# Three moves in a one-core latent-attention kernel: later hooks, another fetch order, and a step's first keys made one step earlier

## The chip, the core and the metric

The kernel runs on one core of a Trainium2 chip. Its time is the device time of one execution in microseconds (us), and less is better. The core has five engines with an instruction queue each: TensorE (PE in the profile, with its weight loads as PEld), VectorE (DVE), ScalarE (ACT), GpSimd (POOL) and SyncE (SP), which here only issues DMAs. A queue is worked off in order, so an instruction that waits holds up all that are behind it on the same engine.

## What is computed

The state x holds 8 batches of 64 tokens with 256 features (512 tokens), float32. The context holds 8 batches of 1601 rows with 128 features. Four levels follow each other, and each adds a cross attention to the context, a self attention and a feed-forward part to the state:

```python
x = x + L0_xattn(layernorm(x), ctx)   # attention a1 over x, an MLP, attention a2 over the context (16 heads of 32), an MLP
x = x + L0_attn(layernorm(x));  x = x + L0_ffn(layernorm(x))     # mixture of 8 experts
x = x + L1_xattn(layernorm(x), ctx, ctx)                         # one head of 256
x = x + L1_attn(layernorm(x));  x = x + L1_ffn(layernorm(x))     # a recurrence; 8 experts with a capacity
x = x + L2_xattn(layernorm(x), ctx)                              # 16 heads of 64
x = x + L2_attn(layernorm(x));  x = x + L2_ffn(layernorm(x))     # mixture of 8 experts
x = x + L3_xattn(layernorm(x), ctx)                              # 16 heads of 16
x = x + L3_attn(layernorm(x));  x = x + L3_ffn(layernorm(x))     # mixture of 16 experts
```

The attention in the first one normalises the context rows, then takes for every head the softmax over the 1601 rows:

```python
yn = _ln(y, lny_g, lny_b)                       # y is the context; per row
a = softmax(einsum('bhsd,bhtd->bhst', q, k) * D ** (-0.5))
o = einsum('bhst,bhtd->bhsd', a, v)             # k and v are projections of yn
```

The last one (L3) is `Q = x @ Wq.T`, `K, V = z @ Wkv.T` of the raw context z, softmax over 1601 keys per head, and `O @ Wo.T`.

## The kernel before

**The stages** follow each other as the reference does. In the texts below, the *first cross attention* is a2 (131 to 568 us), the *second* is x1 (L1, 780 to 840), the *third mixture* is f2 (L2's experts, 1487 to 1581), and the *third cross attention* whose keys the change speaks of is x3 (L3, 1581 to 1897), which the code does with `narrow_attention`. (Between the second one and x3 stands x2 of L2, 990 to 1436, which the change leaves alone.)

**The turned loop** (`turned_attention`) does a2, x2 and x3. It lays keys on partitions and 512 columns (heads times tokens) on the free axis. A batch has 13 key tiles of 128 rows (the last has 65), in pairs 7 chunks (`NCK`), and two halves of the heads, so that a batch takes 14 steps and the whole loop 112 and some more to run out. In step s it does, in this order: the hooks of that step (own work of the stage, given as a dictionary from step to functions), the shift (L808, DVE) and the exponential (L812, ACT) of older chunks, the scores of chunk s (L865, four TensorE records into two one-bank PSUM tiles psS, each copied to SBUF by ScalarE as raw, L866) with a running maximum on VectorE (top, L787), and the sums of the chunk that is `LATE` = 10 steps old (L877, TensorE, 16 records). After a half's last chunk the maximum is turned (psm, L793), reduced (nm, L795) and spread over the keys again (psmb, L802; copy mb, L804, on ScalarE); the shift needs mb. The first sums can run only when the first half's maximum is known. That stretch, some 20 us from step 7 on, is called the fill below. The order is written out by hand (`tc.manual_schedule` on PE, ACT and DVE): the program's order is the order of those queues. POOL and SP go by a scheduler.

**a2's hooks** (L1508 to L1522) prepare batch b+1 while batch b runs, from step 14b on: `stats` in steps 0 to 4 (VectorE), `scales` in step 4 (POOL), `normalise` (L1394, ScalarE, four key tiles of the context in natural layout, cn, in place) in steps 7 to 10, `turn_context` (four TensorE transposes into psc, L1480, and ScalarE's copy to ct, L1482) in steps 9 to 12, the DMA `fetch` of batch b+2 in step 10, and, for two batches at a time (odd b), `ask` in step 12: TensorE's 32 products of the queries with the key weights (psqk, L918), copied by ScalarE (qk, L935). psc, psqk, psm, psmb and the turned answers all come from one PSUM pool `ps` with two buffers. The answers of a half are turned (psot, L898; copy oT, L901) and, per batch, multiplied by the value weights (pso, L1503; copy into qT, L1506).

**x1** (the loop `flash`) takes two batches as a tile, with both layouts of the context (cn natural, ct turned) loaded for each: `fetch(i)` issues cn, ct, cn, ct on SP for tile i, and is called for tile i+1 in tile i's second unit. Scores (L1684) read ct, the sums read cn. The buffers are 4 of each, so two tiles.

**f2** ends with the shared expert's last product (psd, L1140; added to X, L1288) and `collect` (L1283 to L1285): four reads of the answers from DRAM (got, alternately issued by SP and ScalarE), and eight additions into X on VectorE. Weights come by `weight(name)` into a ring of six slots (L314 to L318); a load waits until the slot's last reader is done, so adding a load to the ring changes which reader each later load waits for, and the loads are issued by SP in order.

**x3** takes xn, turns it (L384), projects the queries (psl, L402, copied to qT by ScalarE and VectorE), and then `narrow_attention` sets the value tiles v to one (L949, POOL), loads the turned context of two batches (ct), spreads the queries of batch 0 (`ask`, qz, L957, POOL) and makes the keys of the first half (`key_part(0, n)`, psk, L965, copy kT, L966), all ahead of the loop. Other halves' keys are made by hooks in the loop. Here the loop has one score buffer (psS with four banks, L988, copied by L993) and `late` is 11. The answers go to a tile oT, which the last product (`lin_nat`) reads.

Of the kernel before, what the change touches and what calls it, by code (L numbers as in the profile page):

```python
# [11 lines left out]
F32 = mybir.dt.float32  # L12
# [5 lines left out]
P = 128  # L18
B, S, C = 8, 64, 256
NT = B * S  # L20
# [253 lines left out]
def perceiver(ctx: ExitStack, tc: tile.TileContext, d, col_at, row_at, const_at, out):  # L274
# [46 lines left out]
    def chunks(w, n):  # L321
        return w.rearrange("p (k n) -> p k n", n=n)
# [613 lines left out]

    def narrow_attention(ps, psS, psO, pool, q, wkv, outT):

        hm = K("hp16")
        cts, qzs, kTs, oas = {}, {}, {}, {}
        nk = -(-M // 4)
        vs = [pool.tile([P, KT * 4, 4, 16], F32, tag=f"v{n}", name="v", bufs=1) for n in range(2)]
        for v in vs:
# [99 lines left out]
        fetch(0)  # L1048
        fetch(1)
        ask(0)  # L1050
        for n in range(4):
            key_part(0, n)
        turned_attention(ps, pool, score_part, sum_part, hooks, LATE + 1, 4)


# [57 lines left out]

    def gated_parts(ps, pool, srcT, wg, wu, n, bg=None, bu=None):
        nh = -(-n // P)
        hT = pool.tile([P, nh, NT], F32, tag=f"hT{nh}", name="hT", bufs=1 if nh > 3 else 2)
        kc = C // P
        sgs = tpool.tile([P, 2, NT], F32, tag="T", name="sg")

        def up(c):  # L1120
            m = min(P, n - c * P)
            tg = ps.tile([P, 512], F32, tag="ps", name="psg")
            tu = ps.tile([P, 512], F32, tag="ps", name="psu")
            for w, t in ((wg, tg), (wu, tu)):
                for k in range(kc):
                    nc.tensor.matmul(t[:m], w[:, k, c * P : c * P + m], srcT[:, k, :], start=k == 0, stop=k == kc - 1)  # L1126
            sg = sgs[:, c % 2, :]
            if bg is None:
                nc.scalar.activation(sg[:m], tg[:m], AF.Silu)
                nc.vector.tensor_tensor(hT[:m, c, :], sg[:m], tu[:m], ALU.mult)  # L1130
            else:
                nc.scalar.activation(sg[:m], tg[:m], AF.Silu, bias=bg(c))
                nc.vector.scalar_tensor_tensor(hT[:m, c, :], tu[:m], bu(c), sg[:m], ALU.add, ALU.mult)

        def down(wd, done, tiles=range(NI)):
            for i in tiles:
                t = ps.tile([P, 512], F32, tag="ps", name="psd")
                for c in range(nh):
                    m = min(P, n - c * P)
                    nc.tensor.matmul(t[:, :C], hT[:m, c, i * P : (i + 1) * P], wd[:m, c, :], start=c == 0, stop=c == nh - 1)  # L1140
                done(i, t[:, :C])

        return up, down
# [188 lines left out]
    with tc.tile_pool(name="l0res", bufs=1) as res, ExitStack() as both:  # L1332
# [129 lines left out]
        with tc.tile_pool(name="a2o", bufs=1) as op:  # L1462

            qT = op.tile([P, 4, NT], F32, tag="qT", name="qT")
            with ExitStack() as _:
# [5 lines left out]
                with ps as ps, psS as psS, psO as psO, fp as fp:  # L1471
# [39 lines left out]
                    for b in range(B - 1):  # L1511
                        at = 2 * NCK * b
                        more = {k: [lambda b=b, k=k: stats(b + 1, 3 * k)] for k in range(5)}
                        more[4].append(lambda b=b: scales(b + 1))
                        for k in range(4):
                            more[7 + k] = [lambda b=b, k=k: normalise(b + 1, 4 * k)]
                        for k in range(4):
                            more.setdefault(9 + k, []).append(lambda b=b, k=k: turn_context(b + 1, 4 * k))
                        more[10].append(lambda b=b: fetch(b + 2))
                        if b % 2:  # L1520
                            more[12].append(lambda b=b: ask(b + 1))
                        hooks.update({at + k: v for k, v in more.items()})  # L1522
                    ask(0)
                    for k in range(0, KT, 4):
                        turn_context(0, k)
# [125 lines left out]
    with tc.tile_pool(name="x1", bufs=1) as pool:  # L1651
# [17 lines left out]
        with ps as ps, psS as psS, psO as psO, fp as fp:  # L1669
            ctx_of = {}  # L1670

            def fetch(i):
                for j in range(2):
                    cn = fp.tile([P, KT, CO], F32, tag="cn", name="cn", bufs=4)
                    nc.sync.dma_start(cn.rearrange("p k c -> p (k c)"), d["cn"][2 * i + j])
                    ct = fp.tile([P, M], F32, tag="ct", name="ct", bufs=4)
                    nc.sync.dma_start(ct, d["ct"][2 * i + j])
                    ctx_of[2 * i + j] = cn, ct

            def tile_of(i):  # L1680
                def scores(lo, hi, t):
# [266 lines left out]


    W2 = d["f2w"].shape[2]  # L1950
    weights2 = ExitStack()
    w2 = weights2.enter_context(tc.tile_pool(name="w2", bufs=1)).tile([P, 8 * W2], F32, tag="w2", name="w2")
    wq, wk, wvo = (chunks(weight(k), C) for k in ("b2q", "b2k", "b2vo"))
# [6 lines left out]
    with general() as ps, tc.tile_pool(name="f2", bufs=2) as pool:  # L1960
        wg = chunks(weight("f2g"), 8)
        ww = chunks(weight("f2s"), C)
        b2 = pool.tile([8, C], F32, tag="b2", name="b2", bufs=1)
        nc.sync.dma_start(b2, d["f2b"])
        xn = normed(X)
# [30 lines left out]
        with tc.manual_schedule(engines=FLASH):  # L1996
# [2 lines left out]
                (mybir.EngineType.PE, mybir.EngineType.DVE),  # L1999
            )  # L2000
        down(ww[:, 4:6], into_X, (1, 2, 3))
        collect(pool, shares)
    weights2.close()

    with tc.tile_pool(name="x3", bufs=1) as pool:
        wq, wkv, wo = (weight("x3" + k) for k in ("q", "kv", "o"))
        qT = pool.tile([P, 2, NT], F32, tag="qT", name="qT")
        oT = pool.tile([P, 2, NT], F32, tag="oTall", name="oTall")  # L2010
        with general() as ps:
            xT = transposed(ps, normed(X))
            lin_T(ps, chunks(wq, C), xT, C, lambda c, t: evac(qT[:, c, :], t))
        ps, psS, psO, fp = turned_pools("x3", 1, 1, 3)
        with ps as ps, psS as psS, psO as psO, fp as fp:
            narrow_attention(ps, psS, psO, fp, qT, wkv, oT)
        with general() as ps:
            lin_nat(ps, chunks(wo, C), oT, into_X)

# [68 lines left out]
```

## Time and profile before

| what | value |
| --- | --- |
| median of 3 runs | 2035.22 us (2032.83 to 2038.2) |
| profiled execution | 2034.59 us, of which the span is 2032.8 |
| busy over the span | PE 1836.7 us (90%), DVE 1236.9 (61%), ACT 1037.4 (51%), POOL 270.9 (13%) |
| mean granted TensorE clock | 0.951 |
| a2, 131 to 568 us | PE busy 421.75 of 437 us, ACT 299.76, DVE 296.46 |
| x1, 780 to 840 us | PE busy 49.10 of 60 us, DMA share 0.70 |
| f2, 1487 to 1581 us | PE busy 72.11 of 94 us |
| x3, 1581 to 1897 us | PE busy 278.71 of 316 us, DVE 272.28, ACT 269.40 |

Times of instructions are those of one profiled execution, counted from the start of its span. A line of the timeline gives start, duration, engine, line of the kernel, operation, output and inputs, their shapes, and how many instructions of one kind in a row it stands for; in brackets, how long the engine had been idle before and what released it. "Granted clock" is the share of full speed at which TensorE was clocked.

### The profile page before, as it was taken

What the parts mean: (1) busy time and instruction counts of PE and PEld (TensorE: products, weight loads), DVE (VectorE), ACT (ScalarE), POOL (GpSimd) and SP (SyncE); (2) the same over time, 40 slices, a digit from 0 to 9 for tenths busy, and PEclk for the clock granted to TensorE, in tenths of its full rate; (3) what the DMA queues carried; (4) which work ended last, traced back from release to release, by engine and by line L of the source; (5) the groups of instructions that cost most, each with busy time, mean ns of one, the idle gap of its engine ahead of it and who ended that gap; (6) DMA issues with size and microseconds to landing.
All of it is one profiled execution on the core that took longest, in us unless ns stands there. A gap on an engine that the chain in (4) does not pass through costs nothing.

```text
span 2032.8 us, 35983 instructions
## 1 busy us (share of the span) xinstructions
PE 1836.7 (90%) x14950; PEld 1350.3 (66%) x14950; DVE 1236.9 (61%) x2124; ACT 1037.4 (51%) x1721; POOL 270.9 (13%) x331
## 2 busy tenths in 40 slices
PE   6888999999989898769999999999969699998889
PEld 5546777777768475439657777778845377776747
DVE  6457676766726433661266666665544589999743
ACT  2347777777622222402166555555212499999323
POOL 3431010111022221000000000000122110100124
PEclk9999999999998898869999999999979799999989
DMA  8310000000005206317301010100421110100323
GB/s 309 116 62 1 18 18 18 18 28 1 1 25 219 89 29 269 113 44 256 133 17 34 34 34 34 34 18 7 191 81 40 68 35 19 35 19 17 141 67 106
DMA packets 38227, 142.24 MB, mean 70 GB/s; under 512 B 4936, under 2 KB 17872, under 8 KB 32496
## 3 DMA queue, kind: packets, MB, share of 16 engines
q1 hardware_dynamic: 32448, 127.98, 17.6%
q0 software_dynamic: 3696, 10.11, 1.4%
q8 instruction: 119, 1.95, 0.4%
q10 hardware_dynamic: 1920, 1.84, 0.3%
q14 instruction: 44, 0.36, 0.1%
HBM read 129.28 MB, written 19.71 MB: 73 GB/s over the span
## 4 chain that ended last, share of the span: by engine, by line
PE 66%; DVE 15%; ACT 8%; issue 2%; POOL 2%; DMA 1%; DVEq 0%; ACTq 0%; SPq 0%; POOLq 0%
PE psav L877 17%; PE psS L865 16%; PE psgd L1242 4%; DVE raw L808 4%; DVE top L787 4%; PE psl L402 3%; PE psn L411 2%; PE psy L1263 2%; ACT raw L993 2%; PE psg L1126 2%; PE psh L1867 1%; ACT raw L812 1%; PE psy L1871 1%; PE psu L1126 1%; ACT cn L1394 1%
## 5 line engine op out<-in xcount | busy, mean ns | idle before, releaser
L877 PEld LDWEIGHTS psav<-cn,raw 128*128 128x128 f32 (+1 forms) x3328 | 402.3, 191 | 87.1 <-issue 85.8
L808 DVE TENSOR_TENSOR raw<-raw,mb 128x1024 f32<-128x1024 f32 (+1 forms) x336 | 381.8, 1140 | 62.6 <-ACT mb L804 62.6
L877 PE MATMUL psav<-cn,raw 128*128 128x129 f32 (+1 forms) x3328 | 406.7, 275 | 0.7 <-ACT raw L812 0.7
L865 PE MATMUL psS<-qk,ct 128*128 128x512 f32 (+1 forms) x832 | 396.1, 598 | 7.6 <-ACT raw L866 7.6
L787 DVE TENSOR_TENSOR top<-raw,top 128x1024 f32<-128x1024 f32 (+1 forms) x240 | 267.9, 1116 | 135.6 <-ACT raw L866 111.9
L812 ACT ACTIVATE raw<-raw 128x1024 f32<-128x1024 f32 (+1 forms) x336 | 334.6, 998 | 14.3 <-DVE raw L808 11.9
L866 ACT COPY raw<-psS 128x512 f32<-128x512 f32 (+1 forms) x416 | 236.0, 585 | 132.0 <-PE psS L865 128.7
L865 PEld LDWEIGHTS psS<-qk,ct 128*128 128x128 f32 (+1 forms) x832 | 138.0, 187 | 114.5 <-issue 80.6
L993 ACT COPY raw<-psS 128x1024 f32<-128x1024 f32 (+1 forms) x112 | 106.6, 952 | 4.9 <-PE psS L988 4.8
L988 PE MATMUL psS<-qz,kT 32*128 32x128 f32 (+1 forms) x1664 | 78.0, 298 | 22.6 <-ACT raw L993 22.4
L1242 PE MATMUL psgd<-w,xdT 128*128 x272 | 91.9, 470 | 1.6 <-DVE xdT L1231 1.6
L475 POOL MEMSET vz<- 128x528 f32 (+1 forms) x12 | 7.4, 644 | 612.8 <-PE pso L1924 428.8
L781 DVE TENSOR_TENSOR top<-raw 128x1024 f32<-128x1024 f32 x48 | 58.7, 1222 | 46.1 <-ACT raw L866 35.7
L353 POOL TENSOR_TENSOR mv<-mv,mhalf 128x1 f32<-128x1 f32 x76 | 43.2, 572 | 325.6 <-DVE mv L352 315.0
L988 PEld LDWEIGHTS psS<-qz,kT 32*128 32x128 f32 (+1 forms) x1664 | 55.6, 183 | 46.5 <-ACT raw L993 38.3
L1007 PE MATMUL psav<-raw,v 128*32 128x64 f32 (+1 forms) x3328 | 71.9, 227 | 3.5 <-ACT raw L812 1.8
L804 ACT COPY mb<-psmb 128x512 f32<-128x512 f32 x48 | 28.1, 586 | 75.2 <-PE psmb L802 68.5
L1007 PEld LDWEIGHTS psav<-raw,v 128*32 128x32 f32 (+1 forms) x3328 | 53.5, 112 | 18.4 <-issue 3.3
L974 PEld LDWEIGHTS psv<-w_x3kv_None,ct 128*128 128x128 f32 (+1 forms) x416 | 54.0, 190 | 15.8 <-issue 3.1
L1268 POOL DMA_INDIRECT answered<-rows,homes x53 | 51.0, 963 | 95.5 <-ACT rows L1266 58.8
L1242 PEld LDWEIGHTS psgd<-w,xdT 128*128 128x128 f32 x272 | 48.2, 192 | 21.1 <-issue 8.8
L974 PE MATMUL psv<-w_x3kv_None,ct 128*128 128x128 f32 (+1 forms) x416 | 59.5, 282 | 0.0
(423 smaller groups left out, 2718.9 us busy)
## 6 DMA issues: line engine op xcount, KB each, us to landing
cn<-in_cn_dram SPq DMA_DIRECT2D x24, 838.5 KB, 4.4
ct<-in_ct_dram SPq DMA_DIRECT2D x24, 800.5 KB, 4.5
dealt<-in_deal_dram SPq DMA_DIRECT2D x3, 2955.5 KB, 26.9
w<-in_f0w_dram SPq DMA_DIRECT2D x8, 1088.0 KB, 14.8
w_f1up<-in_f1up_dram SPq DMA_DIRECT2D x8, 1024.0 KB, 4.8
w_f1dn<-in_f1dn_dram SPq DMA_DIRECT2D x8, 1024.0 KB, 4.9
w<-in_f2w_dram SPq DMA_DIRECT2D x8, 1024.0 KB, 14.1
w<-in_f3w_dram SPq DMA_DIRECT2D x16, 384.0 KB, 8.2
```

The lines of the kernel that those rows point to most:

```text
L402: nc.tensor.matmul(t[:m, :NT], w[:, k, c * P : c * P + m], src[:, k, :], start=k == 0, stop=k == kc - 1)
L787: nc.vector.tensor_tensor(top[:n, :m, :], raw, top[:n, :m, :], ALU.max)
L808: nc.vector.tensor_tensor(raw, raw, halves[h]["mb"][:n].unsqueeze(1).to_broadcast([n, m, 512]), ALU.add)
L812: nc.scalar.activation(raw, raw, AF.Exp)
L865: nc.tensor.matmul(x[:n], ct[:, kt * P : kt * P + n], qk, start=True, stop=True)
L866: nc.scalar.copy(raw[:n, i, :], x[:n])
L877: nc.tensor.matmul(oa[:, j // 2, j % 2 * CO : (j % 2 + 1) * CO], w[:n, i, j * P : (j + 1) * P], cn[:n, kt, :], start=kt == 0 and j % 2 == ...
L974: nc.tensor.matmul(t[:n, i * P : (i + 1) * P], cts[b][:, kt * P : kt * P + n], wkv[:, C + c * P : C + (c + 1) * P], start=True, stop=True)
L988: nc.tensor.matmul(x[:n, g, i * P : (i + 1) * P], kTs[h][r, kt * P : kt * P + n], qzs[b][r, c].rearrange("p m s -> p (m s)"), start=True, ...
L993: nc.scalar.copy(raw[:n, :m, :].rearrange("p i (g s) -> p i g s", g=4), x[:n, :, : m * P].rearrange("p g (i s) -> p i g s", s=P))
L1007: nc.tensor.matmul(oa[32 * g : 32 * g + 32, s * S : (s + 1) * S], vs[h % 2][:n, 4 * kt + g, 2 * s : 2 * s + 2, :].rearrange("p s d -> p (s ...
L1242: nc.tensor.matmul(y[:, :m], st[t]["xT"][:, k, :], w[:, bass.ds(x + at + k * m, m)], start=k == 0, stop=k == C // P - 1)
```

## The change

The change has three parts. In a2, the hooks `normalise` and `turn_context` are put three steps later (10 to 13 and 12 to 15 of a batch, so that the last two turns fall in the next batch's first two steps, and the hooks of a step are now extended instead of overwritten). In x1, `fetch` issues both ct of a tile ahead of both cn. For x3, the weights x3kv and the turned context of batch 0 are loaded into the weight ring at the start of f2, the keys of the first half are made at the end of f2, ahead of `collect`, into a tile kT0 of a pool of its own (`early`), and `narrow_attention` takes kT0 in place of making them; it still loads batch 0's context for itself, for the values and the second half's keys. The answers are written into qT itself and the tile oT goes. In `gated_parts` the tile hT has one buffer always, where it had two for f2.

```diff
--- before.py
+++ after.py
@@ -936,13 +936,13 @@
-    def narrow_attention(ps, psS, psO, pool, q, wkv, outT):
+    def narrow_attention(ps, psS, psO, pool, q, wkv, outT, kT0):
         hm = K("hp16")
-        cts, qzs, kTs, oas = {}, {}, {}, {}
+        cts, qzs, kTs, oas = {}, {}, {0: kT0}, {}
         nk = -(-M // 4)
         vs = [pool.tile([P, KT * 4, 4, 16], F32, tag=f"v{n}", name="v", bufs=1) for n in range(2)]
         for v in vs:
@@ -1048,8 +1048,6 @@
         fetch(0)
         fetch(1)
         ask(0)
-        for n in range(4):
-            key_part(0, n)
         turned_attention(ps, pool, score_part, sum_part, hooks, LATE + 1, 4)
@@ -1113,7 +1111,7 @@
     def gated_parts(ps, pool, srcT, wg, wu, n, bg=None, bu=None):
         nh = -(-n // P)
-        hT = pool.tile([P, nh, NT], F32, tag=f"hT{nh}", name="hT", bufs=1 if nh > 3 else 2)
+        hT = pool.tile([P, nh, NT], F32, tag=f"hT{nh}", name="hT", bufs=1)
         kc = C // P
         sgs = tpool.tile([P, 2, NT], F32, tag="T", name="sg")
@@ -1513,13 +1511,14 @@
                         more = {k: [lambda b=b, k=k: stats(b + 1, 3 * k)] for k in range(5)}
                         more[4].append(lambda b=b: scales(b + 1))
                         for k in range(4):
-                            more[7 + k] = [lambda b=b, k=k: normalise(b + 1, 4 * k)]
+                            more[10 + k] = [lambda b=b, k=k: normalise(b + 1, 4 * k)]
                         for k in range(4):
-                            more.setdefault(9 + k, []).append(lambda b=b, k=k: turn_context(b + 1, 4 * k))
+                            more.setdefault(12 + k, []).append(lambda b=b, k=k: turn_context(b + 1, 4 * k))
                         more[10].append(lambda b=b: fetch(b + 2))
                         if b % 2:
                             more[12].append(lambda b=b: ask(b + 1))
-                        hooks.update({at + k: v for k, v in more.items()})
+                        for k, v in more.items():
+                            hooks.setdefault(at + k, []).extend(v)
                     ask(0)
                     for k in range(0, KT, 4):
                         turn_context(0, k)
@@ -1670,12 +1669,14 @@
             ctx_of = {}
             def fetch(i):
-                for j in range(2):
-                    cn = fp.tile([P, KT, CO], F32, tag="cn", name="cn", bufs=4)
+
+                cts = [fp.tile([P, M], F32, tag="ct", name="ct", bufs=4) for _ in range(2)]
+                cns = [fp.tile([P, KT, CO], F32, tag="cn", name="cn", bufs=4) for _ in range(2)]
+                for j, ct in enumerate(cts):
+                    nc.sync.dma_start(ct, d["ct"][2 * i + j])
+                for j, cn in enumerate(cns):
                     nc.sync.dma_start(cn.rearrange("p k c -> p (k c)"), d["cn"][2 * i + j])
-                    ct = fp.tile([P, M], F32, tag="ct", name="ct", bufs=4)
-                    nc.sync.dma_start(ct, d["ct"][2 * i + j])
-                    ctx_of[2 * i + j] = cn, ct
+                    ctx_of[2 * i + j] = cn, cts[j]
             def tile_of(i):
                 def scores(lo, hi, t):
@@ -1948,6 +1949,8 @@
     W2 = d["f2w"].shape[2]
+    early = ExitStack()
+    kT0 = early.enter_context(tc.tile_pool(name="x3e", bufs=1)).tile([P, M], F32, tag="kT0", name="kT0")
     weights2 = ExitStack()
     w2 = weights2.enter_context(tc.tile_pool(name="w2", bufs=1)).tile([P, 8 * W2], F32, tag="w2", name="w2")
     wq, wk, wvo = (chunks(weight(k), C) for k in ("b2q", "b2k", "b2vo"))
@@ -1960,6 +1963,8 @@
     with general() as ps, tc.tile_pool(name="f2", bufs=2) as pool:
         wg = chunks(weight("f2g"), 8)
         ww = chunks(weight("f2s"), C)
+        wkv3 = weight("x3kv")
+        ct0 = weight("ct", 0)
         b2 = pool.tile([8, C], F32, tag="b2", name="b2", bufs=1)
         nc.sync.dma_start(b2, d["f2b"])
         xn = normed(X)
@@ -1999,23 +2004,30 @@
                 (mybir.EngineType.PE, mybir.EngineType.DVE),
             )
         down(ww[:, 4:6], into_X, (1, 2, 3))
+
+        for lo in range(0, M, 401):
+            n = min(401, M - lo)
+            t = ps.tile([P, 512], F32, tag="ps", name="psk")
+            nc.tensor.matmul(t[:, :n], wkv3[:, :P], ct0[:, lo : lo + n], start=True, stop=True)
+            nc.scalar.copy(kT0[:, lo : lo + n], t[:, :n])
         collect(pool, shares)
     weights2.close()
     with tc.tile_pool(name="x3", bufs=1) as pool:
-        wq, wkv, wo = (weight("x3" + k) for k in ("q", "kv", "o"))
+        wq, wo = (weight("x3" + k) for k in ("q", "o"))
         qT = pool.tile([P, 2, NT], F32, tag="qT", name="qT")
-        oT = pool.tile([P, 2, NT], F32, tag="oTall", name="oTall")
         with general() as ps:
             xT = transposed(ps, normed(X))
             lin_T(ps, chunks(wq, C), xT, C, lambda c, t: evac(qT[:, c, :], t))
         ps, psS, psO, fp = turned_pools("x3", 1, 1, 3)
         with ps as ps, psS as psS, psO as psO, fp as fp:
-            narrow_attention(ps, psS, psO, fp, qT, wkv, oT)
+            narrow_attention(ps, psS, psO, fp, qT, wkv3, qT, kT0)
         with general() as ps:
-            lin_nat(ps, chunks(wo, C), oT, into_X)
+            lin_nat(ps, chunks(wo, C), qT, into_X)
+
+    early.close()
```

## The prediction

> **What bounds the kernel now.** I read the chain of waits first, then busy time by stage, then TensorE's waits inside the stages that the edits touch, and last the timelines at the three places.
>
> ```profile
> PE 66%; DVE 15%; ACT 8%; issue 2%; POOL 2%; DMA 1%; DVEq 0%; ACTq 0%; SPq 0%; POOLq 0%
> ```
>
> TensorE carries two thirds of the chain, so an edit pays only where TensorE stands still. The windows (name, then length and the busy time of PE, weight loads, DVE, ACT and POOL, the granted clock, the DMA share, GB/s) show where that is:
>
> ```profile
> 131.00:165.00 34.00, 25.88 (x100) 12.29 (x99) 16.91 (x38) 23.00 (x46) 5.11 (x4) 0.95 0.04 16
> 215.00:482.00 267.00, 262.60 (x1741) 195.05 (x1741) 187.75 (x305) 190.16 (x331) 31.26 (x20) 1.00 0.06 19
> 1573.00:1597.00 24.00, 8.08 (x18) 3.28 (x16) 11.19 (x27) 1.13 (x2) 7.78 (x6) 0.64 0.34 118
> 1597.00:1621.00 24.00, 19.64 (x228) 13.61 (x228) 11.87 (x12) 17.61 (x27) 2.36 (x4) 1.00 0.09 32
> 1621.00:1627.00 6.00, 4.33 (x57) 3.57 (x56) 5.08 (x5) 5.33 (x6) 0.00 (x0) 0.57 0.00 0
> ```
>
> The first cross attention (131 to 568) loses 8.1 us of TensorE in its first 34 us and only 4.4 in the 267 us of its steady state. Ahead of the third cross attention's loop (1573 to 1597) 16 of 24 us are idle. TensorE's waits over the first cross attention (total, times, longest):
>
> ```profile
> PE psS L865 <- ACT raw L866: 5.9, 8, 2.4
> PE psqk L918 <- ACT qk L935: 2.4, 4, 0.8
> PE psqk L918 <- DVE qT L1506: 0.9, 3, 0.3
> ```
>
> The 5.9 are one wait of 1.49, one of 2.40 and six of 0.33: TensorE waiting for ScalarE to empty a score buffer. So the hooks' place matters, but what is to be had is some 6 us.
>
> **Part 1, later hooks in the first cross attention.** No instruction is added or removed; per batch the four normalisations go from steps 7–10 to 10–13 and the four turns from 9–12 to 12–15. Statistics (DVE), scales (POOL), the DMA fetch and the question stay in their steps. Where they lie now, on ScalarE and then on TensorE:
>
> ```profile
> 154.50 1.65 ACT L1394 ACTIVATE cn<-cn,cmv 128x128 f32<-128x128 f32 x4 [3.74 <-DVE nm L795]
> 156.99 0.58 ACT L804 COPY mb<-psmb 128x512 f32<-128x512 f32 x1
> 162.46 1.28 ACT L812 ACT_TABLE_LOAD   x1
> ```
>
> ```profile
> 154.53 0.65 PE L802 MATMUL psmb<-const,nm 128*128 128x128 f32 x4 [0.78 <-DVE nm L795]
> 165.33 1.98 PE L865 MATMUL psS<-qk,ct 128*128 128x512 f32 x4 [2.40 <-ACT raw L866]
> ```
>
> In the fill (the first half's softmax, when nothing older can be summed), ScalarE normalises from 154.50 although psmb is done at 155.18; mb, which releases the whole shift, comes at 156.99. Two more normalisations of 1.65 and a turn copy of 0.76 stand ahead of the table load at 162.46. Without them: mb 155.2–155.8, the shift (DVE 1.22) to 157.0, step 8's copies to 157.2, table load to 158.5, exponential (1.06) to 159.5, step 9's copies to 160.4. The first copy ends early enough that step 10's scores start near 160.0 instead of 165.33: −5.3. Two sets of turning transposes lay in TensorE's idle time there (159.40 and 162.33) and come later, on the path, at 0.44 each (their spacing): +0.9. Net −4.4. Ends: −5.3 if they find idle time again, −3.0 if only the two waits go (1.49 + 2.40 − 0.9).
>
> Steady state: per step TensorE has scores 1.72 and sums 1.79 (3.5, spacings), 0.44 more with a turn. ScalarE has an exponential and two copies (about 2.0), 1.55 more with a normalisation, 0.77 with a turn or an answer's copy. The six stalls of 0.33 stand in step 10 of a batch, where a normalisation, a turn and that copy meet; after, the normalisations of steps 10 to 13 meet 3.5 to 4.1 us of ScalarE work against 3.5 to 4.5 of TensorE's. I take the stalls as gone, −2.0, with 0 as the other end.
>
> The question in step 12 of three batches (224, 330 and 436 us) is what pays for it. Before, ScalarE reaches it with a lead: at 224.12 the last, short turn copy (0.41) had waited 1.43 for TensorE. After, a normalisation (1.55) and a full turn copy (0.77) stand ahead of it on ScalarE, the turn's psc and the question's psqk share two PSUM buffers, and TensorE's queue is in order: the scores of step 12 wait behind the question. Extra work ahead: 1.55 + 0.36 = 1.9; if the lead of 1.43 were still there, 0.5 would show; if it is gone, 1.9. Steps 10 and 11 now have a normalisation each, so the lead is mostly gone: 1.4 each, +4.2 (ends +1.5 and +5.7).
> Part 1: −4.4 − 2.0 + 4.2 = **−2.2**.
>
> **Part 2, fetch order in the second cross attention.** Of each pair of batches both ct are issued ahead of both cn. The queue moves 410 to 430 GB/s without a gap from 782 to 799 us, so order changes who lands first and not the sum. But the first tile's ct had landed: its scores start at 795.23 with 0.41 put down to issue, and the second tile's wait is for ScalarE:
>
> ```profile
> 802.00 2.63 PE L1684 MATMUL psS<-ct,qk 128*64 128x512 f32 x8 [2.16 <-ACT P L678]
> ```
>
> TensorE waits for no DMA between 778 and 840. cn comes 0.8 MB later per ct moved ahead, about 2 us each, and is first read after two softmax units, several us on. SP is also moved past one f1 weight load (800.69 to about 815, used near 917). 0; ends −0.4 (that issue gap) and +0.5 (a cn just late).
>
> **Part 3, the first keys behind the third mixture.** Four products with x3kv (eight matmul records) and four ScalarE copies move from the front of the third cross attention to the third mixture's end; the oT tile goes (answers are written into qT, whose query readers on POOL are long done: 0).
>
> ```profile
> 1597.14 2.94 PE L965 MATMUL psk<-ct,w_x3kv_None 128*128 128x401 f32 x8 [0.72 <-issue]
> 1597.14 2.36 POOL L957 TENSOR_SCALAR qz<-qT,const 128x128 f32<-128x128 f32 x4 [7.75 <-ACT qT L340]
> 1600.01 0.73 PE L988 MATMUL psS<-qz,kT 32*128 32x128 f32 x16
> ```
>
> With the keys gone the first scores don't start at 1597.1: POOL's qz stands there. Two of its four instructions (0.59 each) give 1598.4. So 2.94 leave TensorE, 1.6 leave the path: **−1.6**. The rest of the fill repeats at ScalarE's cadence (one psS buffer: 0.73, then the copy of 1.01, 1.86 a step) and just moves.
>
> At the new place TensorE is idle from 1573.3 to 1585.6, ScalarE all but idle, so the 2.94 and 4 × 0.5 are covered; without that cover they would be the same 2.9 again. What is not free are the queues that they pass:
>
> ```profile
> 1574.43 0.87 SPq L1283 DMA_DIRECT2D got<-answered  x2
> 1574.55 0.90 ACTq L1283 DMA_DIRECT2D got<-answered  x2
> 1578.25 3.25 DVE L1285 SCALAR_TENSOR_TENSOR X<-got,m,X 128x256 f32<-128x256 f32 x8 [4.52 <-DMA got<-answered]
> 1581.61 2.87 POOL L949 MEMSET v<- 128x3328 f32 x1 [8.84 <-DVE X L1285]
> 1585.06 0.94 DVE L357 TENSOR_SCALAR xn<-X,mv 128x256 f32<-128x256 f32 x2 [1.56 <-POOL mv L353]
> ```
>
> On ScalarE a copy of 0.5 now stands between its two issues of got, and one X addition needs the second of them. Two early tiles (x3kv and ct) shift the ring of weight slots, so that the 512 KB of b3vo are released by the last psd (1573.3) and are queued on SP ahead of got: 1.2 us at 420 GB/s, in front of 1 MB that the eight additions take in one by one until 1581.5. POOL's memset waits for the last of these, and pow and xn for the memset, so a late X passes on whole. Ends: 0 (DMA spreads; DVE works 3.25 us anyhow) and +1.7 (0.5 + 1.2); I take +0.6, as the first 0.5 shows and the transfer mostly lies behind DVE's own time. The early ct and x3kv ride behind the mixture's weights, issued from 1435.6 to 1470 and needed at 1573: 0. The weights pushed back in the ring, b3qk above all, still come before use: 0.
>
> The last cost is TensorE's clock. It was 0.50 from 1578 to 1594, 1.00 from then on, and fell again at 1621 (0.57 over 6 us; a psS group took 1.24 instead of 0.73) after steps in which TensorE was busy 1.87 of 3 us with no wait over 1.67. Without psk TensorE stands idle for 1.9 us at 1596.5 and is then busy in 40% of its first steps, so that the clock may fall early: one drop of 6 us with steps of 2.4 instead of 1.86 costs 1.7, against 0. I take 0: at 1601 to 1606 it held at 1.00 with 1.8 of 3 us busy.
> The Trainium skill ("TensorE: Matmul & The Clock Gate", Part 1: The HAM clock gate) has the clock fall after an idle window of about 3.4 us, so it would put the price of the 1.9 us gap at 0; the drop at 1621 came without any such gap, so the rule does not exclude it here.
> Part 3: −1.6 + 0.6 = **−1.0**.
>
> **Sum.** Against the profiled execution (2034.59: span 2032.8 and 1.8 around it; 0.6 under the median of 2035.22): −2.2 + 0 − 1.0 = −3.2, so 2031.4. That is 0.16%, and 0.3% (6.1 us) is about what a measurement of this kernel can tell from no change.
>
> **Rivals.**
> *Full gain* (2026.6): the question costs nothing more and got is not delayed: −4.4 − 2.0 − 1.6 = −8.0. For it: the steady state has 190 of 267 us on ScalarE, so that a backlog of 1.9 could be eaten elsewhere. Against it: TensorE's order is fixed, and a stall at the question isn't made up.
> *ScalarE becomes the bound of steps 12 and 13* (2042.3): there a normalisation and a turn give it about 4.2 against TensorE's 3.95, with raw released late from step 10 on. If the backlog, once there, exposes one normalisation of 1.55 in each of seven batches, that is +10.9: −3.2 + 10.9 = +7.7. It decides from the point where ScalarE's work of steps 10 to 13 passes TensorE's, about 16 us together. Against it: before, the same four-step train met the same loop and left 0.33 a batch.
> *Nothing shows* (2034.6): the fill's gain is given back, as the late transposes and turns delay the second batch's first scores, and the clock takes the 1.6.
>
> **How the numbers follow.** Forecast 0.49 (own range 2028.5 to 2034.5, from the ends above), full gain 0.28, ScalarE bound 0.13, nothing 0.10. Faster by over 0.3% (below 2028.5 on the profiled scale) is the full gain, 0.28; slower (above 2040.7) most of the ScalarE case, 0.11; the rest, 0.61, is within. The range from 2025.5 to 2038.0 leaves out the ScalarE case and the far side of the full gain, under 0.2.
>
> **What would show it.** Right: the table load near 157, step 10's scores near 160; at 224, 330 and 436 psqk waits of over 1 us on ScalarE; no psS wait of 0.33 in step 10; no psk at the third cross attention's front and psS 1.3 us behind qT; 778 to 840 unchanged. Wrong: psS waits on raw in steps 12 and 13 of every batch, a DMA wait ahead of X grown by over 1.7, a clock under 1.00 between 1596 and 1615, or a difference in a stage that no edit touches.

## The result, and the profile after

The changed kernel takes 2049.74 us (median of 5 runs, 2044.74 to 2050.7) against 2035.22 for the kernel before: a ratio of 1.0066 (95% interval 1.0053 to 1.0079), slower by 0.66%, some 13 us. The profiled execution took 2047.1, with a span of 2045.3 and a mean granted TensorE clock of 0.943 (0.951 before). The forecast was 2031.4, with a range of 2025.5 to 2038.0.

Where the 12.5 us of the span lie is read by taking the same TensorE instruction in both traces and subtracting its start. The difference is +1.0 us ahead of the first cross attention, −4.4 at 170 us (the fill's gain), +4.2 at that stage's end, +6.9 at 597 us and again +1.8 from 698 us to the second cross attention, +4.2 through the whole loop between 1010 and 1474 us, +3.9 ahead of the reads of the answers in the third mixture, +6.5 at the turning of xn behind them, +10.2 at 1613 us, +9.2 from 1630 us, +11.7 at the start of the next attention. Two places that the edits touch hold most of the loss: the first cross attention behind its fill, and the stretch from the third mixture's end through the third cross attention.

Between 568 and 780 us the difference also moves, up by 2.7 and down by 5.1, though nothing was edited there. Both moves lie where only one of the two traces records half speed of TensorE: 585.4 to 592.2 us in the new trace; 628.6 to 635.4 and 655.9 to 659.3 in the old. A difference in a stage that no edit touches was among the signs of being wrong.

In windows (length, busy time of PE, weight loads, DVE, ACT and POOL, granted clock, DMA share, GB/s):

```profile
131.00:165.00 34.00, 27.72 (x114) 13.23 (x113) 19.26 (x40) 21.95 (x42) 5.10 (x4) 1.00 0.05 16
215.00:482.00 267.00, 261.48 (x1698) 194.02 (x1697) 181.59 (x300) 185.41 (x320) 31.26 (x20) 0.97 0.05 16
1606.00:1619.70 13.70, 11.33 (x102) 8.48 (x98) 4.84 (x4) 6.38 (x8) 0.76 (x2) 0.50 0.07 27
```

The fill has 1.8 us more of busy TensorE time. Its clock is 1.00 where it had been 0.95 (half speed from 157.6 to 161.0 us); that can't have been worth much, as ScalarE, on whose copies TensorE waits there, had no gap of its own before from 154.50 to 165.66. The steady state, where the clock had been 1.00, shows 0.97; the front of the third cross attention's loop 0.50 for 13.7 us, where it had been 1.00.

The fill, on ScalarE and then on TensorE:

```profile
156.21 0.58 ACT L804 COPY mb<-psmb 128x512 f32<-128x512 f32 x1 [2.65 <-PE psmb L802]
158.53 1.28 ACT L812 ACT_TABLE_LOAD   x1
```

```profile
161.41 1.98 PE L865 MATMUL psS<-qk,ct 128*128 128x512 f32 x4 [1.72 <-ACT raw L866]
```

mb follows psmb directly, the table load comes four microseconds sooner, and of the two waits of 1.49 and 2.40 one of 1.72 is left. That is as forecast. The waits of TensorE over the first cross attention are not:

```profile
PE psqk L918 <- DVE qT L1504: 3.7, 3, 1.2
PE psqk L918 <- ACT qk L935: 2.1, 4, 0.8
PE psS L865 <- ACT raw L866: 1.7, 1, 1.7
```

The six stalls of 0.33 are gone. The wait at the questions has grown from 0.9 to 3.7, and it is for VectorE. One question, ScalarE, VectorE and TensorE, first in the kernel before (TensorE alone):

```profile
224.37 1.36 PE L918 MATMUL psqk<-qT,w_a2wk_None 64*128 64x128 f32 x16 [0.29 <-DVE qT L1506]
226.27 1.71 PE L918 MATMUL psqk<-qT,w_a2wk_None 64*128 64x128 f32 x16 [0.54 <-ACT qk L935]
227.91 1.98 PE L865 MATMUL psS<-qk,ct 128*128 128x512 f32 x4
```

and now:

```profile
217.97 1.04 ACT L866 COPY raw<-psS 128x512 f32<-128x512 f32 x2
218.91 1.65 ACT L1392 ACTIVATE cn<-cn,cmv 128x128 f32<-128x128 f32 x4
219.05 1.23 DVE L787 TENSOR_TENSOR top<-raw,top 128x1024 f32<-128x1024 f32 x1 [2.66 <-ACT raw L866]
220.19 0.42 DVE L1504 COPY qT<-pso 128x256 f32<-128x256 f32 x1
220.66 1.78 PE L918 MATMUL psqk<-qT,w_a2wk_None 64*128 64x128 f32 x16 [1.22 <-DVE qT L1504]
222.99 2.58 PE L918 MATMUL psqk<-qT,w_a2wk_None 64*128 64x128 f32 x16 [0.54 <-ACT qk L935]
225.49 2.73 PE L865 MATMUL psS<-qk,ct 128*128 128x512 f32 x4
```

A normalisation in step 11 makes ScalarE's copies of raw late, the running maximum (DVE, 219.05) waits 2.66 us for them, the copy of the answer into qT stands behind that maximum on VectorE, and the question stands behind that copy. And then the scores at 225.49 take 2.73 us instead of 1.98: TensorE has been put to half speed.

```profile
216.80:220.20 3.40, 2.65 (x50) 2.20 (x48) 1.15 (x2) 3.40 (x8) 0.00 (x0) 1.00 0.00 0
220.20:223.60 3.40, 2.19 (x20) 1.62 (x20) 1.54 (x3) 2.25 (x6) 0.00 (x0) 1.00 0.00 0
223.60:227.00 3.40, 3.40 (x16) 2.50 (x17) 0.00 (x0) 1.81 (x5) 0.00 (x0) 0.50 0.00 0
```

TensorE is busy for 2.19 of 3.40 us, and in the next 3.4 us it is clocked at one half. The same happens at the other two questions, at 329 and 439 us, for 6.8 us each.

At the third mixture's end (SP, DVE) and the third cross attention's front (PE):

```profile
1577.14 0.35 SPq L318 DMA_DIRECT2D w_b3vo_None<-in_b3vo_dram  x1
1578.27 0.88 SPq L1281 DMA_DIRECT2D got<-answered  x2
...
1583.82 1.00 DVE L1283 SCALAR_TENSOR_TENSOR X<-got,m,X 128x256 f32<-128x256 f32 x2 [6.25 <-DMA got<-answered]
1585.20 2.07 DVE L1283 SCALAR_TENSOR_TENSOR X<-got,m,X 128x256 f32<-128x256 f32 x5 [0.38 <-DMA got<-answered]
1587.19 0.42 DVE L349 BATCH_NORM_STATS2 st<-X 128x6 f32<-128x256 f32 x1
1587.53 0.47 DVE L1283 SCALAR_TENSOR_TENSOR X<-got,m,X 128x256 f32<-128x256 f32 x1
```

```profile
1605.65 0.95 PE L988 MATMUL psS<-qz,kT 32*128 32x128 f32 x16 [1.98 <-POOL qz L957]
...
1611.01 1.24 PE L988 MATMUL psS<-qz,kT 32*128 32x128 f32 x16
```

The first addition now starts 5.55 us behind the first got's issue, where it had been 3.82, and the last one comes with a further wait of 0.38 and behind a BNStats; xn is 2.6 us late. The query projection behind it takes 0.8 us longer, 6.26 instead of 5.49, as half speed lasts 20.5 us there and not 17.1. The first scores do start 1.6 us sooner behind qT than before, TensorE waits 1.98 us for qz, and its clock falls at 1606.0.

### The profile page after: what moved, and what is told of

Read it like the earlier page. It is cut to its first block, busy times and chain, and to the rows that moved or that the text cites. A ratio compares the mean times of both kernels' runs of the same rounds, so it can differ in the third digit from the quotient of the medians.

```text
span 2045.3 us, 36016 instructions
## 1 busy us (share of the span) xinstructions
PE 1847.8 (90%) x14950; PEld 1357.1 (66%) x14950; DVE 1237.1 (60%) x2124; ACT 1037.4 (51%) x1721; POOL 270.4 (13%) x331
## 4 chain that ended last, share of the span: by engine, by line
PE 67%; DVE 15%; ACT 6%; issue 2%; POOL 2%; DMA 2%; SPq 0%; ACTq 0%; DVEq 0%; POOLq 0%
PE psav L877 18%; PE psS L865 17%; PE psgd L1240 4%; DVE raw L808 4%; DVE top L787 3%; PE psl L402 3%; PE psn L411 2%; PE psy L1261 2%; ACT raw L993 2%; PE psh L1868 1%; PE psy L1872 1%; PE psg L1124 1%; PE psqk L918 1%; ACT raw L812 1%; PE psu L1124 1%
```

## The experiments

Unread products, named filler below, change no result. A kernel's number is the ratio of its time to that of the kernel before, measured beside it, and in brackets the 95% interval; 0.1% is 2.0 us.

### Each part alone

`e1_hooks` has the diff's hunk on hooks alone, `e2_keys` those on `narrow_attention`, `gated_parts`, f2 and x3, `e3_fetch` that on `fetch`.

> Part 1 of the change alone (later hooks in the first cross attention). Theory A, the three questions: the fill gains 5.4 us as in the changed kernel, and each question costs TensorE about 2 us more of waiting plus a fall of its clock to one half for 3.4 to 6.8 us (1.7 to 3.4 us lost): -5.4 + 3 x 4 = about +6 us at the end of that stage, less where the clock falls for one window only; total +3 to +6 us. Theory B, clock phases: the loss in this stage is a matter of where the free-running clock windows lie in one execution; then the median of the runs shows -2 to 0 us.

> Part 3 alone (first keys of the third cross attention made at the end of the third mixture). Theory A: the reads of the answers land about 2.6 us late behind b3vo, the front gains 1.6, TensorE's clock falls to one half at the front of the loop for 10 to 14 us, which costs 4 us more than before's own fall later: +5 us in all, with the granted clock near 0.5 in the 14 us behind the first scores. Theory B, clock phases: the fall at the front is one execution's luck: +1 us, clock 1.00 there in this run.

> Part 2 alone (both turned contexts ahead of both natural ones in the second cross attention). Theory A: no wait of TensorE there is for a DMA, 0 us (within 1.5). Theory B: the second cross attention of the changed kernel lost 1 to 2 us between 822 and 845 us because cn lands late; then +1 to +2 us, and a wait for cn in that stage.

The hooks alone: 1.0021 (1.0011 to 1.0031), +4.3 us. The keys alone: 1.0029 (1.0019 to 1.0038), +5.9 us. The fetch order alone: 0.9997 (0.9988 to 1.0007), nothing. The sum is +0.47% against 0.66 (0.53 to 0.79) for the whole; the intervals meet, so that the parts add up as far as this can tell. The hooks' profile shows the clock's falls at 223, 329 and 438 us again and the same waits. From 140 us, ahead of the fill, to its end that stage loses 3.2 us (+0.6 to +3.8; the gains of this stage below are counted in the same way): the fill gives −4.0 (−4.9, of which 0.9 go back as the two late turns are made on the path), the six stalls −2.0, so by this sum the three questions cost 9.2, or 3.1 each. (The profiled execution was the fastest of twelve: at its end it is only 0.9 us late, as stages that it did not edit gave 2.9 back.) The profile of the keys alone shows the clock at 1.00 over the loop's front, 1599 to 1613 us, without a filler: the fall there is not in every execution. xn is 2.5 us late in it too. The third mixture up to the reads of the answers, with its two added loads and hT in one buffer, takes 0.3 us more.

### Later hooks where there is no question

Of this edit, the lines that place the hooks:

```diff
-                            more[7 + k] = [lambda b=b, k=k: normalise(b + 1, 4 * k)]
+                            more[(7 if b else 10) + k] = [lambda b=b, k=k: normalise(b + 1, 4 * k)]
-                            more.setdefault(9 + k, []).append(lambda b=b, k=k: turn_context(b + 1, 4 * k))
+                            more.setdefault((9 if b else 12) + k, []).append(lambda b=b, k=k: turn_context(b + 1, 4 * k))
```

> Hooks of the first batch alone three steps later, those of the other batches as before. There is no question in the first batch, so theory A (the questions cost) expects the fill's gain of 5.4 us whole and no clock fall at the questions: -5 us. Theory B (it's the later steps' load on ScalarE in every batch, or clock phases): -5 us as well for the stage if only the load counts, 0 to -3 in the total if what is gained is given back by clock windows in the stages behind.

0.9975 (0.9964 to 0.9985), −5.1 us. The stage gains 4.1 us, the clock is 1.00 from 215 to 482 us, the questions wait 0.9 for qT as before. The gain of the fill is real, and it stays when the questions are left in peace.

The same with `b % 2` for `b` in the condition, so that all batches without a question are late:

> Later hooks in the batches without a question (0, 2, 4, 6), the others as before. Theory A (the loss is the questions' alone): the fill's 5.4 us as with the first batch alone, three more stalls of 0.33 gone, no clock fall: -5 to -6.5 us against before. Theory B (late turns cost TensorE time in any batch, as two sets of transposes move onto the path of the next batch): 0.4 to 0.9 us lost again in each of the three further batches, -3 us.

0.9983 (0.9972 to 0.9994), −3.5 us: three more stalls of 0.33 are gone (psS waits for raw 4 times, 2.7 in all), but the clock fell once, at 329 us, and the stage gains no more than with the first batch alone. The interval doesn't part the two theories.

### The question one step later, and a filler ahead of it

```diff
-                            more[12].append(lambda b=b: ask(b + 1))
+                            more[13].append(lambda b=b: ask(b + 1))
```

> Later hooks alone, and the question one step later (13 in place of 12), so that a step's scores and sums lie between the answer's products and the question. Theory A (the question waits for VectorE's copy of the answer, 3.7 us in all, and the clock falls because TensorE stands idle there): the wait for qT goes, the granted clock stays at 1.00 from 215 to 482 us, and the stage ends 6 to 8 us ahead of the kernel before: -5 to -7 us. Theory B (the question's place does not matter: ScalarE's backlog of steps 10 to 13 is what TensorE meets): waits of the same sum turn up as scores waiting for raw or qk, the clock falls again, and the total stays at +3 to +5 us.

0.9989 (0.9980 to 0.9997), −2.2 us, a gain, though less than the 5 to 7 us of theory A: the wait for qT is gone, and the hooks alone at 1.0021 have become a gain. What is left at the question is a wait for the turn's copy (1.4 in all) and one fall of the clock, at 436 us. The filler in `ask`, with the question in step 12:

```diff
+                        if b:
+                            x = psS.tile([P, 512], F32, tag="S", name="psfill")
+                            nc.tensor.matmul(x, cts[b - 1][:, :P], qks[b - 1].rearrange("p h s -> p (h s)")[:, :512], start=True, stop=True)
```

> Later hooks alone with the question left in step 12, and one product of scores (512 columns, nobody reads it) added ahead of each of the three questions, which fills some 0.9 us of TensorE's wait of 1.2. No work of use is added, and the question starts no earlier. Theory A (the clock's fall is caused by that idle time and is most of the loss, about 6 us of 9): the clock stays at 1.00 from 215 to 482 us, the total is 5 to 6 us below that of the later hooks alone: about -1 to -2 us against before. Theory B (the stall itself is the loss, the clock's fall a side show): no change against the later hooks alone, +4 us.

```profile
219.64 1.02 PE L1489 MATMUL psfill<-qk,ct 128*128 128x512 f32 x2
221.03 1.78 PE L918 MATMUL psqk<-qT,w_a2wk_None 64*128 64x128 f32 x16 [0.37 <-DVE qT L1509]
```

The question starts no earlier, yet the stage's loss of 3.2 us became a gain of 1.9 in the profile: two of the three falls of the clock are gone, the first is still there. Over the runs it is 1.0004 (0.9988 to 1.002), with 8 runs at 2027.7 to 2033.9 and 4 at 2041.5 to 2042.8: the mean granted clock was 0.950 to 0.953 in the eight and 0.946 or 0.947 in the four. It seems that the filler removes the falls in some executions and not in all; the trace is of one of the eight. So idle time at the question does set the clock, and the clock is the larger part of a question's price. Both together:

> All hooks later, the question in step 13, and ahead of each question one product of 512 columns that nobody reads (0.9 us). Theory A (the wait at the question, 0.5 for the turn's copy and 0.5 to 0.8 for the first copies, still lets the clock fall in some executions): no fall from 215 to 482 us, so the runs come closer together, and the median is 0 to 2 us below that with the question in step 13 alone (-2): -2 to -4. Theory B (the filler only takes time): three times 0.4 us more, -1.

0.9970 (0.9961 to 0.9980), 2029.45 us against 2034.98: the fastest here, with 9 runs within 2.1 us. The clock is 1.00 from 215 to 482 us, and the stage gains 6.3 us.

```profile
215.00:482.00 267.00, 264.79 (x1757) 196.16 (x1756) 189.07 (x306) 191.81 (x335) 31.26 (x20) 1.00 0.05 16
```

### The early keys: the ring's order, the front's clock, the end

```diff
-    wqk, wvo = chunks(weight("b3qk"), C), chunks(weight("b3vo"), C)
+    wqk, wg3, wvo = chunks(weight("b3qk"), C), chunks(weight("f3g"), 17), chunks(weight("b3vo"), C)
...
-        wg = chunks(weight("f3g"), 17)
+        wg = wg3
```

> The early keys alone, with one edit: the 17 KB f3g are taken from the weight ring ahead of the 512 KB b3vo, so that b3vo waits for the early keys and is issued behind the reads of the answers (got). Theory A (b3vo ahead of got is what delays X by 2.5 us): the turning of xn at the third cross attention's front is 0 to 0.5 us late instead of 2.5, and the total is 2 to 2.5 us below that of the early keys alone: +3 to +4 us against before, as the clock's share stays. Theory B (the early copies on ScalarE between its two issues of got, or the changed order of the X additions, delay X): the front is 2 us late or more as before, and the total unchanged at +6.

```profile
1574.73 0.88 SPq L1281 DMA_DIRECT2D got<-answered  x2
1576.29 0.35 SPq L318 DMA_DIRECT2D w_b3vo_None<-in_b3vo_dram  x1
```

With b3vo behind got, xn is 0.15 us late instead of 2.5, though the copy between ScalarE's two issues is still there: the transfer queued ahead was the delay. The total did not follow, 1.0032 (1.0021 to 1.0044): in this profile the clock fell at the loop's front (10.2 us of half speed from 1601.5), and the end was slow. A filler of two products at the front of the loop:

```diff
         ask(0)
+        for n in range(2):
+            t = ps.tile([P, 512], F32, tag="ps", name="psfill")
+            nc.tensor.matmul(t[:, :401], wkv[:, :P], cts[0][:, :401], start=True, stop=True)
```

> As the early keys with f3g ahead of b3vo, and two products of keys (401 columns, nobody reads them) put at the front of the third cross attention's loop, where TensorE waits 2 us for POOL's qz. Theory A (the clock falls at the front in many executions because TensorE stands idle there): the median is 2 to 4 us below that without the filler, -1 to +1 against before. Theory B (the clock's fall there is not tied to that idle time): no difference from the kernel without the filler.

1.0022 (1.0013 to 1.0031). No profile of a kernel with this filler (three, with those below) shows a fall at the front, and two of the three without it do. In the window of 3.41 us ahead of those two falls TensorE was busy for 1.44 and 1.57 us; with a filler no window at full clock in the loop's first 10 us had less than 2.1. (In the third profile one with 1.47 us, directly behind a rise of the clock, was not followed by a fall.) The 2 us between the totals are inside the intervals. It is still slower than before, by 4.5 us, and its loop stands only 0.8 us behind before at 1870 (2.0 of loss in the third mixture, most of it seen in this profile alone, are partly made up by then), so there is a loss later: at the loop's end, where TensorE drains. That 25 us of the kernel before, and then of this one:

```profile
1875.00:1900.00 25.00, 17.95 (x366) 14.15 (x359) 19.53 (x40) 11.60 (x16) 3.35 (x11) 0.80 0.09 31
```

```profile
1876.80:1901.80 25.00, 18.14 (x323) 14.72 (x324) 17.38 (x33) 10.70 (x14) 2.64 (x10) 0.66 0.10 31
```

Nearly the same stretch of the loop, at a clock of 0.66 instead of 0.80; 17.1 us of half speed instead of 10.2 over the whole end. All six profiles of kernels with early keys have 13.6 to 17.1 us of it there, and the eleven others 6.8 to 10.2. Is it the answers written in place?

> The kernel before with one edit of the early keys alone: the third cross attention's answers are written into qT and the tile oT goes. Theory A (the clock's phase): 0 us within 1.5, clock at that stage's end as before (10 us of one half). Theory B (the edit itself slows the end): +2 us or more, 17 us of half clock there.

1.0006 (0.9996 to 1.0016): not at the end (6.8 us of half speed). It is slower by 0.07 us in each batch, which the kernels with early keys show too; 0.5 us in all. Is it where the loop lies among the clock's windows? Three and four filler products behind the keys of the kernel before (`range(3)`, `range(4)`), and four instead of two in the kernel with early keys:

> The kernel before with three products of keys (401 columns, 0.73 us each, nobody reads them) added behind the first keys of the third cross attention: its loop starts 2.2 us late, and nothing else is changed. Theory A (at that stage's end TensorE's clock stays at one half for 17 us instead of 10 because the loop has been moved against the clock's 3.41 us windows, as in every kernel with the early keys): the moved phase is that of the early keys with the filler, so the stage's end shows 17 us of half clock and the total is 2.2 + 2 = about +4 us. Theory B (the longer half clock at the end comes from the early keys' other edits, the answers in place or the tiles): +2.2 us, and the end's clock as before.

> The kernel before with four products that nobody reads behind the first keys of the third cross attention in place of three: 0.73 us more. Theory A (phase): the loop's end is moved to the place among the clock's windows that the kernels with early keys have (2.6 to 3.3 us behind a boundary), with 17 us of half clock there, and the total is 0.7 + 2 us above that with three products: +5 to +6.5 against before. Theory B: 0.7 us above it, +3.5 to +4.5, and 10 us of half clock at the end.

> The early keys with f3g ahead of b3vo and with four products that nobody reads at the loop's front in place of two: 1.47 us more of TensorE's time there, nothing else. Theory A (phase): the loop's end is moved to a place among the clock's windows (about 1.8 us behind a boundary) where the kernel before has 10 us of half clock and not 17, so the 2 us lost at the end come back and the total is that of two products less 0 to 1 us: +3 to +4 against before, in spite of the added 1.47. Theory B (the end is slow for another reason): 1.5 us more than with two products, +5.5.

Three: 1.0019 (1.0010 to 1.0027). Four: 1.0021 (1.0012 to 1.0030); its loop runs 4.4 us late (1.6 of it from ahead of the stage), and 1.1 of that come back at the end, with 6.8 us of half speed, where three products lost 0.8 there. So one product of 0.73 us more ahead of the loop changed the time of an unchanged end by 2 us, but the other way than I expected. (In these two profiles the ends lie 1.65 us apart, not 0.73, as the clock's fall near 1625 was 3.4 us long in the one and 6.8 in the other.) Early keys with four: 1.0021 (1.0011 to 1.0031), the same as with two, though it has 1.47 us more to do. In its profile the loop runs 1.0 to 1.4 us ahead of before up to 1862, as before's own clock fall at 1622 is missing there, and the end and the last mixture take back 1.7 and 2.1.

Which place is bad can be read from all seventeen profiles. The clock's changes lie on a grid of 3.41 us; take the instruction that stands at 1862 us in the kernel before, its distance from the grid's last point, and the time from there to the start of the next attention against that of the kernel before. At 0.86 us (four products) that time is 1.3 us shorter. At 1.1 to 1.7 us, where nine kernels lie, the kernel before among them, it is the same within 0.1. At 2.2 to 3.4 us it is longer: by 0.75 with three products (2.17 us), and by 1.7 to 2.2 in the six kernels with early keys. So the end goes with its place on the grid, and early keys have a slow one at least partly because all six lie in its later part. Place is not all of it: at the same 2.17 us the early keys alone lose 2.2. What the rest is stays open.

### All mended

The changed kernel with the question in step 13, its filler, the ring's order and two fillers at the loop's front:

> The changed kernel with its found losses mended: question in step 13 with one unread product ahead, f3g ahead of b3vo in the weight ring, two unread products at the front of the third cross attention's loop. If the parts add up: -5.5 to -6 (later hooks so mended) and +4 (early keys so mended) and 0 (fetch order) give -1 to -2 us against before, some 15 us below the changed kernel. If the 3 to 4 us by which the whole change was slower than the sum of its parts come from the parts acting on each other, +2 us.

0.9992 (0.9983 to 1.0001): 2033.02 us, 15 us under the changed kernel by the two ratios. The parts add up: −6.1 and +4.5 make −1.6, and it is −1.6 (−3.5 to +0.2). So what was mended is the changed kernel's loss, but for the 4.5 us that the early keys still cost and whose cause is only in part known (some 2 at the loop's end, 0.5 from the answers in place).

## Why the prediction was wrong, point by point

The ends that the prediction's steps name add up to 2026.8 and 2039.6, so even with every term at its slow end the sum stays 7 to 10 us below what was measured: terms were missing, or bounded too low.

**The fill** (−4.4) was right: −4.0, by the steps given, table load and scores where they were expected. **The six stalls** (−2.0) were right, and are gone. **The fetch order** (0) was right.

**The question** (+1.4 each) is the first step that failed: 3.1 each. The wait itself grew by 0.9 each, less than I took, but on another way, over the maximum and VectorE's queue: I had counted what stands ahead on ScalarE and not followed it into the queue of the engine that copies the answer. The other 2.2, what is left of the 3.1, go with TensorE's clock, a term that I had priced only for the third cross attention; with the filler, which took two falls of 6.8 us away, the stage came out 5.1 us shorter. At the question TensorE waits twice within 3.4 us; 0.6 to 0.8 us less of busy time there was enough.

**The clock at the third cross attention's front** was bounded at 0 to 1.7 and taken as 0. Over its 13.7 us of half speed the changed kernel lost 4.5 us (+5.65 to +10.18), of which 1.0 came back as before's own later fall was shorter. The bound was wrong because I let the clock fall for one stretch of 6 us (which by its own steps, 2.4 in place of 1.86, is 1.35 and not 1.7): it stayed at half for four windows of 3.41 us, with TensorE busy for 11.33 of the 13.70. Why it did not rise sooner the runs do not show. The sign for it, a clock under 1.00 between 1596 and 1615, was among those named.

**The reads of the answers** (+0.6, at most 1.7) took 2.5. The bound was 0.5 for ScalarE's copy and 1.2 for the transfer. The copy cost next to nothing: with b3vo behind got and the copy still in its place, xn was 0.15 late. The transfer alone put the first addition 1.7 later, and the last one waits once more and has a BNStats ahead, 0.7 together. **The front** (−1.6) came as forecast: −1.6 behind qT.

**The loop's end** was in no step: +1.7 to +2.2 in the profiles with early keys.

The rival that ended slower (ScalarE as the bound of steps 12 and 13 in every batch) was not what happened: no batch without a question lost anything. The Trainium skill ("TensorE: Matmul & The Clock Gate", Part 1: The HAM clock gate) lets the clock fall after an idle window of about 3.4 us. The length agrees with the stretches of 3.4 and 6.8 us seen here; the condition does not. The clock's changes lie on a grid of 3.41 us. Of the grid's windows in which TensorE, at full clock, was busy for less than 2.95 us between 175 and 480 us, worked out from the records of all seventeen profiles, nine had 2.05 to 2.52 us of busy time, and each was followed by half speed; forty-six had 2.58 to 2.92, and none was. So there the limit lies at three quarters of busy time, not at none. It is another one elsewhere. In the fill of the same stage, 138 to 175 us, ten windows with 0.59 to 1.59 us were followed by half speed, and none of those with 1.63 or more. At the third cross attention's front, 1597 to 1640 us, it was eighteen with 1.44 to 1.85, and none with 1.99 or more (the one with 1.47 named above was not).

## What to carry to other kernels

Moving work to another step of a hand-ordered loop must be followed through every in-order queue up to the next serial exchange between engines (here answer, copy, question, copy): work that is harmless in a step full of independent products is late work where TensorE waits for one copy. Where TensorE is the bound, price a new wait twice: its own length, and up to half of the 3.4 to 6.8 us that follow, if it leaves TensorE too little busy over 3.4 us (here less than three quarters between the first cross attention's products, about half in its fill: read the limit from your own trace, stage by stage); a product that nobody reads, put into the wait, can be worth more than its time. Adding a tile to a ring of weight slots re-orders the loads behind it: look for which large load is now queued ahead of a read that somebody waits for.

## What the runs showed of the hardware that I had not expected

TensorE's clock fell behind windows of 3.41 us in which TensorE was busy for up to 2.52 us. That limit holds for the first cross attention's steady state alone: in its fill it lay at 1.6 us, in the second cross attention the clock fell behind a window with 3.01 us of busy time, over half of it products with a single column (psb, L1666), and in attention a1, near 65 us, it held behind 1.5 to 2.3, so busy time is not the whole condition. A stage's time depends on where it lies on the grid: the drain at the third cross attention's end, the same instructions, came out 2 us apart in the kernels with three and with four added products. The runs of one kernel spread by 2 us (9 runs of the fastest) to 15 us (12 runs with the filler in step 12); that the grid makes this spread is likely, but not shown.
